# A graph layer with residual and layer norm on one core: one PSUM tile per bank, a relu on each of two engines, register loads behind long operations, 101 copied groups

## The chip, the core and the metric

The kernel runs on one core of a Trainium2 chip. The metric is the device time of one execution in microseconds, here 1737.42 us as the median of three runs (1736.82 to 1737.85). The engines are named as in the profile: PE (matmul), PEld (its weight load), DVE (vector), ACT (scalar), POOL (GpSimd) and SP (sync, which only issues transfers).

## What is computed

The reference is one step of message passing over 12500 nodes of 64 values and 200000 edges of 32 values, then a residual and a layer norm. `col` (the destinations, `dst`) is sorted.

```python
msg_in = jnp.concatenate([nodes[row], nodes[col], edge_features], axis=-1)
messages = relu(msg_in @ mW1 + mb1) @ mW2 + mb2
aggregated = jax.ops.segment_sum(messages, col, num_segments=12500)
upd_in = jnp.concatenate([nodes, aggregated], axis=-1)
x = _layernorm(x + relu(upd_in @ uW1 + ub1) @ uW2 + ub2)
```

All of it is float32. mW1 is 160x128, mW2 128x64, uW1 128x128 and uW2 128x64.

## The kernel before

The edges are cut into 1563 tiles of 128. Six tiles make a group, here called a step: there are 261 steps (0 to 260), and two of them make a super-group g. A step's number is s, and j is 0 or 1 for the first or second step of its super-group.

**Sources.** The product of all nodes with the first 64 rows of mW1 is written to a table in DRAM early on (`tab_a`). For each tile POOL gathers the 128 rows of its sources from that table with one indirect transfer (line 209) into a ring of nine buffers `xg`. The first ten steps gather x itself and are transposed and multiplied. POOL's gathers are issued in the order of the steps, each as soon as its buffer is free.

**Copied groups.** In the steps of the list `COPIED` only four of the six tiles are gathered. The x columns of the sources of the other two tiles are copied inside SBUF, one column at a time, into a tile `xc` (64 rows for each tile), and PE multiplies them with mW1's rows (line 370). 96 steps are copied before: 16, 19, 21, 24 and so on, every 2.5 steps to 254. For each of the 128 columns a register holds the address in `xtop`, another that in `xbot`. ACT makes 64 of the 128 columns (`singly`, line 338, an add through the bias), DVE the other 64 (`joined`, line 345, a bitwise or). The addresses come from SBUF by register loads (`addresses`, line 315), at most eight columns at a time, on the same engine's queue. The work for a copied step is spread evenly over the 2.5 steps before it, and in a step DVE's part is split in two (j = 1) or three (j = 0) portions at fixed places in the order.

**Destinations and edges.** PE multiplies, for each tile, a 64-row operand `l` (32 rows of a one-hot selection of destinations, 32 of edge features) with `rhs` (32 rows of the destination table `tab_b`, 32 of mW1) into the PSUM tile `pc` (line 367). `select` makes the one-hot rows on DVE (lines 235 and 237) and a second selection `sel` (line 243) once per super-group. 

**The step.** `node_part(s)` adds the gathered rows to `pc` on DVE into `h` (line 394; line 390 in a copied step, four tiles only), and ACT applies the relu (lines 395, 391 and 392). Then `collect(s-1)` sums h by destination with PE into `sums` (line 427) and counts edges (line 424), `edge_part(s+1)` fills the next `pc`, and DVE and ACT make their portions of copies. `pc` is a tile of two PSUM banks, with two buffers.

**Updates.** 34 times in the run a period of up to 448 nodes is closed: ACT copies `sums` (lines 441, 442), SP loads the x columns of its nodes (`columns`, line 457), PE multiplies (`update`, lines 464, 465, and `residual`, lines 478, 480), ACT applies the relu (line 470), and DVE and ACT do the layer norm (lines 494 to 510). `update` and `residual` each take a buffer of `pc`. The last period begins at step 258. For it `columns` is called in step 260, at the place of the other calls, and its transfer stands behind those that SP has been given before.

The order of instructions on every engine is the order in which this code writes them; nothing is reordered.

Of the kernel before, what the change touches and what calls it, by code (L numbers as in the profile page):

```python
# [17 lines left out]
P = 128  # L18
# [6 lines left out]
SUB = 6  # L25
# [47 lines left out]
FIRST, GAPS = 16, (3, 2)  # L73
COPIED = []
while FIRST + sum(GAPS) * (len(COPIED) // len(GAPS)) + sum(GAPS[:len(COPIED) % len(GAPS)]) < NSUB - 6:
    COPIED.append(FIRST + sum(GAPS) * (len(COPIED) // len(GAPS)) + sum(GAPS[:len(COPIED) % len(GAPS)]))
RNDS = -(-len(COPIED) // len(GAPS))
LAST = 4 * (N - 1)
ACTS, CHUNK = 64, 8
# [22 lines left out]
def gnn_kernel(ctx: ExitStack, tc: tile.TileContext, x1T, x, eT, e_rows, src, src_row, dst, dst_row, wlist, wrow, wnext, whalf,  # L102
# [40 lines left out]

    cols = const.tile([RNDS * len(GAPS), 2 * P], I32, name="cols")
    col_a = const.tile([RNDS * len(GAPS), P, 2], I32, name="col_a")
# [68 lines left out]
    with tc.tile_pool(name="sup", bufs=2) as sup, tc.tile_pool(name="work", bufs=2) as work, tc.manual_schedule():  # L214
# [73 lines left out]
        def columns_list():  # L288

            for r in range(len(GAPS)):  # L290
                v = src_row[:, ((FIRST + sum(GAPS[:r])) * SUB + SUB - 2) * P:]
                nc.sync.dma_start(cols[r * RNDS:(r + 1) * RNDS],
                                  bass.AP(v.tensor, v.offset, [[sum(GAPS) * SUB * P, RNDS], [1, 2 * P]]))
            cv = cols.rearrange("k (b e) -> k b e", b=2)
            for b, base in enumerate((XBASE, YBASE)):
                nc.vector.tensor_scalar(col_a[:, :, b], cv[:, b], 4.0, float(base), op0=ALU.mult, op1=ALU.add)
# [3 lines left out]
        def portion(s, total, unit):  # L300

            rate, found = sum(GAPS) / len(GAPS), []
            begin = min(c - 2 - (j + 1) * rate for j, c in enumerate(COPIED[:len(GAPS)]))
            for j, c in enumerate(COPIED):
                lo, hi = (min(-(-int(total * (s + d - begin - j * rate) / rate * 16 + 0.5) // (16 * unit)) * unit, total) for d in (0, 1))
                lo = max(lo, 0)
                if lo < hi:
                    if c not in xc:
                        xc[c] = work.tile([P, P], F32, name="xc")
                    found.append((xc[c], j % len(GAPS) * RNDS + j // len(GAPS), lo, hi))  # L310
            return found

        def addresses(k, a, m, engine):

            _, v = nc.values_load_multi_w_load_instructions(  # L315
                col_a.rearrange("k e b -> k (e b)")[k:k + 1, 2 * a:2 * m], engines=[engine], min_val=XBASE,
                max_val=YBASE + LAST, skip_runtime_bounds_check_because="sources are node numbers")
# [15 lines left out]
        def singly(s, part, of):  # L333

            todo = [(o, k, e) for o, k, lo, hi in portion(s, ACTS, 2) for e in range(lo, hi, 2)]
# [4 lines left out]
        def joined(s, part, of):  # L340

            todo = [(o, k, ACTS + e) for o, k, lo, hi in portion(s, P - ACTS, 2) for e in range(lo, hi, 2)]
            for o, k, a, m in share(todo, part, of):
                for e, top, bot in addresses(k, a, m, ET.DVE):
                    nc.vector.tensor_tensor(o[:, e:e + 1].bitcast(I32), top.bitcast(I32), bot.bitcast(I32),  # L345
                                            op=ALU.bitwise_or)
# [9 lines left out]
        def edge_part(s):  # L356

            n = len(tiles(s))
            g, j = divmod(s, SUP // SUB)

            pc = psum.tile([P, 2, 4, DH], F32, name="pc")[:, :, :SUB // 2]
            for i in range(n):
                k, b = divmod(i, 2)
                q, m = 64 * b, j * SUB // 2 + k
                w = m if shared(g) == 1 else (j * SUB + i) // shared(g)
                copied = s in COPIED and i >= SUB - 2
                nc.tensor.matmul(pc[:, b, k, :], L[g][q:q + 64, m, :], rhs[g % 2][q:q + 64, w, :],  # L367
                                 start=s >= XG or k == 0, stop=s >= XG and not copied)
                if copied:
                    nc.tensor.matmul(pc[:, b, k, :], xc[s][q:q + 64], w1a[q:q + 64], start=False, stop=True)  # L370
            pcs[s] = pc

        def node_part(s):
# [3 lines left out]
            h = work.tile([P, 2, SUB // 2, DH], F32, name="h")  # L377
            if s < XG:
                xt = xs.pop(s)
                for i in range(n):  # L380
                    k, b = divmod(i, 2)
                    q = 64 * b
                    nc.tensor.matmul(pc[:, b, k, :], xt[q:q + 64, k, :], w1a[q:q + 64], start=False,
                                     stop=i + 2 >= n)
                nc.scalar.activation(h, pc, AF.Relu)
            else:
                a = xg.pop(s)[0].rearrange("p (b k) f -> p b k f", b=2)
                if s in COPIED:
                    m = SUB // 2 - 1
                    nc.vector.tensor_tensor(h[:, :, :m], pc[:, :, :m], a[:, :, :m], op=ALU.add)  # L390
                    nc.scalar.activation(h[:, :, :m], h[:, :, :m], AF.Relu)  # L391
                    nc.scalar.activation(h[:, :, m:], pc[:, :, m:], AF.Relu)
                for b, m in parts(n) if s not in COPIED else []:
                    nc.vector.tensor_tensor(h[:, b, :m], pc[:, b, :m], a[:, b, :m], op=ALU.add)  # L394
                    nc.scalar.activation(h[:, b, :m], h[:, b, :m], AF.Relu)  # L395
# [9 lines left out]
        def collect(s):  # L405
# [20 lines left out]
            for i in range(n):  # L426
                nc.tensor.matmul(ps[:, bass.ds(ws[i], WIN)], h[:, i % 2, i // 2, :], S[g][:, k0 + i, :],  # L427
# [46 lines left out]
        def residual(u):  # L474

            py = psum.tile([P, UB, D], F32, name="py", tag="sums" if u + 2 == K else "pc")
# [91 lines left out]
        def products(c, w):  # L568
            pb = psum.tile([P, 2, HB, DH], F32, name="pb", tag="pc")
            for i in range(HB):  # L570
                for h, m in spread(c):
                    if i < m:
                        nc.tensor.matmul(pb[:, h, i, :], (xbot if h else xtop)[64 * h:64 * h + 64, (c + HB * h + i) * P:(c + HB * h + i + 1) * P],  # L573
# [3 lines left out]
        def chunk_a(c):  # L577
            pb, tb = products(c, w1a)
            for h, m in spread(c):
                if h:  # L580
                    nc.vector.tensor_copy(tb[:, h, :m], pb[:, h, :m])  # L581
                else:
                    nc.scalar.copy(tb[:, h, :m], pb[:, h, :m])  # L583
# [3 lines left out]
        def chunk_b(c, into):  # L587
            pb, tb = products(c, w1b)
            n = min(NCH, NB - c)
            pf, tf = (t.rearrange("p h i f -> p (h i) f")[:, :n] for t in (pb, tb))  # L590
            nc.vector.tensor_tensor(tf, pf, b1.unsqueeze(1).broadcast_to([P, n, DH]), op=ALU.add)
# [107 lines left out]
        def weights():  # L699

            pw = psum.tile([D, DH], F32, name="pw", tag="pc")
# [3 lines left out]
            pw2 = psum.tile([DH, DH], F32, name="pw2", tag="pc")  # L705
            nc.tensor.matmul(pw2, w2T, u1a, start=True, stop=True)
            nc.vector.tensor_copy(w2u, pw2)
            pw3 = psum.tile([1, DH], F32, name="pw3", tag="pc")
# [3 lines left out]
        def checks():  # L712
# [15 lines left out]
            pf = psum.tile([1, 1], F32, name="pf", tag="pc")  # L728
# [27 lines left out]
        for s in range(last + 2):  # L756
# [13 lines left out]
            if s < NSUB:  # L770
                node_part(s)
                joined(s, 0, 3 if j == 0 and g + 1 < NSUP else 2)
# [54 lines left out]
    with tc.If(flag > 0), tc.tile_pool(name="gen", bufs=1) as up:  # L827
# [28 lines left out]
        with tc.For_i(0, NT, 1) as t:  # L856
# [26 lines left out]
            pc = psum.tile([P, DH], F32, name="pcg", tag="pc")  # L883
# [34 lines left out]
        with tc.For_i(0, NB, 1) as c:  # L918
# [7 lines left out]
            ph = psum.tile([DH, P], F32, name="phu", tag="pc")  # L926
# [66 lines left out]
```

## Time and profile before

| | before |
|---|---|
| time, median of three runs | 1737.42 us |
| time of the profiled execution | 1741.59 us |
| its span, first to last instruction | 1739.8 us |
| granted TensorE clock, mean | 0.581 |
| PE busy | 1448.5 us, 83% |
| PEld busy | 1247.5 us, 72% |
| DVE busy | 1056.2 us, 61% |
| ACT busy | 1468.6 us, 84% |
| POOL busy | 1301.0 us, 75% |
| gathers on POOL (line 209) | 1371 |
| copies on ACT (line 338) and DVE (line 345) | 6144 each |
| register loads on DVE and ACT (line 315) | 1055 and 912 |

The span is counted from the first to the last instruction; 1.8 us of the profiled execution lie around it. The profiled execution took 4.2 us more than the median of the runs. Busy time leaves out register loads, waits on semaphores and the issue of transfers, which an engine's sequencer does. In the tables of groups the numbers behind the bar are the busy time of the group, the mean of one instruction in ns, and the idle time of the engine just before, with what ended it. "issue" stands for idle time that ended without any wait in the profile.

### The profile page before, as it was taken

How to read it: one execution, taken by the hardware profiler on the slowest of the kernel's cores; microseconds unless marked ns; L12 is line 12 of the kernel's file. 1: busy time of each engine (PE TensorE's matmuls, PEld its weight loads, DVE VectorE, ACT ScalarE, POOL GpSimd, SP SyncE). 2: the span in 40 equal slices, each digit the busy share in tenths (PEclk: the TensorE clock that was granted, in tenths of full speed). 3: DMA queues.
4: the chain of work that ended last, by engine and by line, in shares of the span. 5: the costliest groups of instructions: out<-in, count | busy, mean ns of one | idle time of the engine just before them, and what ended most of it. 6: DMA issues, size and time to landing. Idle time of an engine off the chain costs nothing.

```text
span 1739.8 us, 46406 instructions
## 1 busy us (share of the span) xinstructions
PE 1448.5 (83%) x9620; PEld 1247.5 (72%) x9620; DVE 1056.2 (61%) x7329; ACT 1468.6 (84%) x6712; POOL 1301.0 (75%) x1380
## 2 busy tenths in 40 slices
PE   3697888888988888887987898888899878899997
PEld 3586777877777767666776776677777767677776
DVE  1526666666665656666665666666667666666643
ACT  0277989999998898998898999998999999899942
POOL 7777777777777777777777777777777777777774
PEclk8585555555555555656555555655556566666656
DMA  8783444433333333333343433443344444443442
GB/s 213 204 175 99 127 112 115 115 97 100 98 101 92 96 97 93 98 102 94 98 107 102 105 108 103 105 107 103 106 106 110 107 109 106 108 112 104 113 112 66
DMA packets 207588, 192.45 MB, mean 111 GB/s; under 512 B 57511, under 2 KB 173409, under 8 KB 207313
## 3 DMA queue, kind: packets, MB, share of 16 engines
q0 software_dynamic: 43872, 87.97, 20.6%
q1 hardware_dynamic: 148896, 92.56, 19.6%
q10 hardware_dynamic: 14546, 8.93, 1.8%
q8 instruction: 91, 1.49, 0.4%
q14 instruction: 183, 1.50, 0.3%
HBM read 171.54 MB, written 17.76 MB: 109 GB/s over the span
## 4 chain that ended last, share of the span: by engine, by line
POOL 41%; issue 24%; DMA 14%; DVE 10%; PE 5%; ACT 2%; DVEq 2%; SPq 1%; ACTq 0%; POOLq 0%
POOL xg L209 41%; DMA xg<-tab_a,src_s 10%; DVE xc L345 3%; DVE h L394 2%; ACT xc L338 2%; PE sums L427 2%; DVEq L315 2%; PE pc L367 1%; DVE l L237 1%; DMA tab_a<-tb 1%; DMA l<-in_dst_row 1%; DMA w1b<-in_mW 1%; DVE h L390 0%; DMA l<-in_eT 0%; DMA xtop<-in_x1T 0%
## 5 line engine op out<-in xcount | busy, mean ns | idle before, releaser
L209 POOL DMA_INDIRECT xg<-tab_a,src_s x1311 | 1242.0, 947 | 399.8 <-issue 372.0
L338 ACT ACTIVATE xc<-xtop,xbot 128x1 f32 x6144 | 1166.2, 280 | 42.2 <-issue 31.7
L345 DVE TENSOR_TENSOR xc<-xtop,xbot 128x1 int32 x6144 | 536.6, 154 | 417.9 <-issue 402.4
L427 PE MATMUL sums<-sel,h 128*128 128x32 f32 x3126 | 638.9, 371 | 20.4 <-ACT h L395 13.9
L427 PEld LDWEIGHTS sums<-sel,h 128*128 128x128 f32 x3126 | 605.3, 294 | 39.1 <-ACT h L395 15.4
L367 PE MATMUL pc<-rhs,l 64*128 64x128 f32 x3126 | 420.0, 415 | 188.7 <-DVE h L394 134.7
L367 PEld LDWEIGHTS pc<-rhs,l 64*128 64x128 f32 x3126 | 349.6, 295 | 253.0 <-DVE h L394 152.3
L395 ACT ACTIVATE h<-h 128x768 f32<-128x768 f32 x156 | 129.6, 831 | 111.6 <-DVE h L394 110.8
L394 DVE TENSOR_TENSOR h<-pc,xg 128x768 f32<-128x768 f32 x156 | 148.0, 949 | 121.8 <-DMA xg<-tab_a,src_s 67.6
L237 DVE TENSOR_TENSOR l<-l,cps 128x768 f32<-128x768 int32 (+1 forms) x134 | 127.8, 953 | 23.4 <-DMA l<-in_dst_row 18.8
L424 PEld LDWEIGHTS <-one 128*1 128x1 bf16 x1563 | 55.9, 83 | 58.7 <-issue 50.7
L424 PE MATMUL cnt<-sel,one 128*1 128x32 bf16 x1563 | 89.2, 187 | 0.4 <-issue 0.3
L390 DVE TENSOR_TENSOR h<-pc,xg 128x512 f32<-128x512 f32 x96 | 66.1, 688 | 25.8 <-DMA xg<-tab_a,src_s 11.5
L243 DVE TENSOR_TENSOR sel<-cps,drc 128x384 f32<-128x384 f32 x131 | 71.6, 547 | 14.9 <-PE sums L427 14.7
L464 PE MATMUL pu<-xw,uz 128*128 128x448 f32 (+1 forms) x68 | 61.8, 1012 | 17.3 <-DVE h L394 13.6
L370 PE MATMUL pc<-w1a,xc 64*128 64x128 f32 x384 | 75.0, 398 | 0.0
L209 POOL DMA_INDIRECT xg<-in_x,src_s x60 | 58.0, 967 | 19.1 <-issue 17.7
L391 ACT ACTIVATE h<-h 128x512 f32<-128x512 f32 x96 | 59.2, 617 | 10.4 <-DVE h L390 9.5
L370 PEld LDWEIGHTS pc<-w1a,xc 64*128 64x128 f32 x384 | 66.7, 311 | 0.0
L583 ACT COPY tb<-pb 128x512 f32<-128x512 f32 (+1 forms) x13 | 7.4, 570 | 58.5 <-DMA tab_a<-tb 26.1
L465 PE MATMUL pu<-sums_s,w2u 128*128 128x448 f32 (+1 forms) x68 | 55.2, 914 | 0.0
L573 PE MATMUL pb<-w1a,xtop 64*128 64x128 f32 x100 | 24.0, 425 | 29.9 <-DVE tb L581 17.9
(104 smaller groups left out, 803.3 us busy)
## 6 DMA issues: line engine op xcount, KB each, us to landing
l<-in_dst_row SPq DMA_DIRECT2D x262, 96.0 KB
l<-in_eT SPq DMA_DIRECT2D x262, 96.0 KB
xg<-tab_a,src_s POOLq DMA_INDIRECT x1311
rhs<-tab_b SPq DMA_DIRECT2D x361, 32.0 KB
tab_b<-tb SPq DMA_DIRECT2D x13, 512.0 KB
rhs<-tab_b SPq DMA_DIRECT2D x387, 16.0 KB
tab_a<-tb ACTq DMA_DIRECT2D x12, 512.0 KB
out<-y SPq DMA_DIRECT2D x33, 128.0 KB
```

What stands on the lines that cost most here:

```text
L209: nc.gpsimd.indirect_dma_start(out=a[:, i, :] if s < XG else a[:, i // 2, i % 2, :], out_offset=None, in_=A[:, :] if s >= XG else x[:, :], ...
L237: nc.vector.tensor_tensor(l[r], l[r].bitcast(I32), node[r].unsqueeze(2).broadcast_to([r.stop - r.start, SUP // 2, P]), op=ALU.is_equal)
L243: nc.vector.tensor_tensor(s[:, :nt], slot.unsqueeze(1).broadcast_to([P, nt, WIN]), drc[:, g * SUP:g * SUP + nt].unsqueeze(2).broadcast_to( ...
L338: nc.scalar.activation(o[:, e:e + 1], top.bitcast(F32), AF.Identity, bias=bot.bitcast(F32))
L345: nc.vector.tensor_tensor(o[:, e:e + 1].bitcast(I32), top.bitcast(I32), bot.bitcast(I32), op=ALU.bitwise_or)
L367: nc.tensor.matmul(pc[:, b, k, :], L[g][q:q + 64, m, :], rhs[g % 2][q:q + 64, w, :], start=s >= XG or k == 0, stop=s >= XG and not copied)
L370: nc.tensor.matmul(pc[:, b, k, :], xc[s][q:q + 64], w1a[q:q + 64], start=False, stop=True)
L390: nc.vector.tensor_tensor(h[:, :, :m], pc[:, :, :m], a[:, :, :m], op=ALU.add)
L394: nc.vector.tensor_tensor(h[:, b, :m], pc[:, b, :m], a[:, b, :m], op=ALU.add)
L395: nc.scalar.activation(h[:, b, :m], h[:, b, :m], AF.Relu)
L424: nc.tensor.matmul(pn[:, bass.ds(ws[i], WIN)], one, SB[g][:, k0 + i, :, 1], start=False, stop=ends and i == n - 1)
L427: nc.tensor.matmul(ps[:, bass.ds(ws[i], WIN)], h[:, i % 2, i // 2, :], S[g][:, k0 + i, :], start=False, stop=ends and i == n - 1)
```

## The change

- The list of copied groups follows a curve, `progress`, rather than fixed gaps: 0.43 groups a step at first and 0.41 at the end. It gives 101 steps (16, 18, 20, 23 to 254). The work for them runs from step 11 to step 251.
- ACT makes 66 of the 128 columns, DVE 62. There are three buffers of `xc`. The addresses of all steps are prepared, where before only those of copied steps were.
- `pc` becomes two tiles of one bank, `pc0` and `pc1`, and `h` two tiles of half the size. DVE adds each half by itself. ACT applies the relu to the first half, DVE (a `tensor_scalar` with max) to the second. In the second half, and in copied steps in the first, the sum stays in PSUM and the relu writes h.
- DVE's register loads are taken apart from its copies (`fetch` and `join`): four columns are loaded right behind each add (two behind the second one in a copied step) and behind the relu, eight behind line 237, four behind the second selection; what is left of a step's columns follows at the step's end, eight at a time.
- The update takes `pc0`, the residual `pc1`; the products for the tables take one of each. The addition of the bias to the second table is split by bank.
- `columns` of the last period is called at the end of step 258, no longer in step 260.

```diff
-FIRST, GAPS = 16, (3, 2)
+BEGIN, FINAL = 11, 255
+RATES = 0.43, 0.41
+SWING = 0.0
+def progress(s, early=0.0):
+    s = max(s + 1 - BEGIN, 0)
+    return s * (RATES[0] + (RATES[1] - RATES[0]) * s / (2 * NSUB)) + (early if s else 0.0)
...
+for s in range(NSUB):
+    while min(progress(s), progress(s, -SWING if s % 2 else SWING)) >= len(COPIED) + 1 and s + 3 < FINAL:
+        COPIED.append(s + 3)
...
-ACTS, CHUNK = 64, 8
+ACTS, CHUNK = 66, 8
...
             if at is not None:
-                joined(at, 1, 3)
+                join(fetch(quota(at), 8))
             s = sup.tile([P, SUP, WIN], F32, name="sel")
...
+            if at is not None:
+                join(fetch(quota(at), 4))
...
+        def fetch(todo, n):
+            ready = []
+            while todo and n:
+                o, k, a = todo[0]
+                m = min(len([t for t in todo if t[1] == k]), n // 2)
+                del todo[:m]
+                n -= 2 * m
+                ready += [(o, *x) for x in addresses(k, a, a + 2 * m, ET.DVE)]
+            return ready
...
-            pc = psum.tile([P, 2, 4, DH], F32, name="pc")[:, :, :SUB // 2]
+            pc = [psum.tile([P, 4, DH], F32, name=f"pc{b}")[:, :SUB // 2] for b in range(2)]
...
-                if s in COPIED:
-                    m = SUB // 2 - 1
-                    nc.vector.tensor_tensor(h[:, :, :m], pc[:, :, :m], a[:, :, :m], op=ALU.add)
-                    nc.scalar.activation(h[:, :, :m], h[:, :, :m], AF.Relu)
-                    nc.scalar.activation(h[:, :, m:], pc[:, :, m:], AF.Relu)
-                for b, m in parts(n) if s not in COPIED else []:
-                    nc.vector.tensor_tensor(h[:, b, :m], pc[:, b, :m], a[:, b, :m], op=ALU.add)
-                    nc.scalar.activation(h[:, b, :m], h[:, b, :m], AF.Relu)
+                m = SUB // 2 - (s in COPIED)
+                todo = quota(s)
+                if n == SUB:
+                    o = pc[0] if s in COPIED else h[0]
+                    nc.vector.tensor_tensor(o[:, :m], pc[0][:, :m], a[:, 0, :m], op=ALU.add)
+                    nc.scalar.activation(h[0], o, AF.Relu)
+                    ready = fetch(todo, 4)
+                    nc.vector.tensor_tensor(pc[1][:, :m], pc[1][:, :m], a[:, 1, :m], op=ALU.add)
+                    ready += fetch(todo, 2 if s in COPIED else 4)
+                    nc.vector.tensor_scalar(h[1], pc[1], 0.0, None, op0=ALU.max)
+                    join(ready + fetch(todo, 4))
...
-            pu = psum.tile([DH, UN], F32, name="pu", tag="pc")[:, :n]
+            pu = psum.tile([DH, UN], F32, name="pu", tag="pc0")[:, :n]
...
-            if s + 2 in due:
+            if s + 2 in due and due[s + 2] + 1 < K:
                 columns(due[s + 2])
+            if s == UPD[K - 1]:
+                columns(K - 1)
             rest(s)
-            joined(s, 2 if j == 0 and g + 1 < NSUP else 1, 3 if j == 0 and g + 1 < NSUP else 2)
+            while s < NSUB and quota(s):
+                join(fetch(quota(s), CHUNK))
             singly(s, 0, 1)
```

More of the change, by code (lines that the diff above doesn't have):

```diff
@@ L142, in gnn_kernel @@
     past = const.tile([1, 1], F32, name="past")
-    cols = const.tile([RNDS * len(GAPS), 2 * P], I32, name="cols")
-    col_a = const.tile([RNDS * len(GAPS), P, 2], I32, name="col_a")
+    col_a = const.tile([P, 2, P, 2], I32, name="col_a")
     w1b = const.tile([P, DH], F32, name="w1b")
@@ L288, in columns_list, with portion @@
         def columns_list():
[L290 to L296, printed above, removed]
+            cols = work.tile([P, 2, 2, P], I32, name="cols", tag="tb")
+            for r in range(2):
+                n = min(P, NSUB - 1 - r * P)
+                v = src_row[:, (r * P * SUB + SUB - 2) * P:]
+                nc.sync.dma_start(cols[:n, r].rearrange("k b e -> k (b e)"),
+                                  bass.AP(v.tensor, v.offset, [[SUB * P, n], [1, 2 * P]]))
+                for b, base in enumerate((XBASE, YBASE)):
+                    nc.vector.tensor_scalar(col_a[:n, r, :, b], cols[:n, r, b], 4.0, float(base), op0=ALU.mult, op1=ALU.add)
         x8, y8 = xtop.bitcast(U8), xbot.bitcast(U8)
-        def portion(s, total, unit):
-            rate, found = sum(GAPS) / len(GAPS), []
-            begin = min(c - 2 - (j + 1) * rate for j, c in enumerate(COPIED[:len(GAPS)]))
+        def portion(s, total, early=(0.0, 0.0)):
+            found = []
             for j, c in enumerate(COPIED):
-                lo, hi = (min(-(-int(total * (s + d - begin - j * rate) / rate * 16 + 0.5) // (16 * unit)) * unit, total) for d in (0, 1))
-                lo = max(lo, 0)
+                lo, hi = (min(max(int((progress(s + d, early[d + 1]) - j) * total / 2 + 1e-6) * 2, 0), total) for d in (-1, 0))
                 if lo < hi:
                     if c not in xc:
-                        xc[c] = work.tile([P, P], F32, name="xc")
-                    found.append((xc[c], j % len(GAPS) * RNDS + j // len(GAPS), lo, hi))
+                        xc[c] = work.tile([P, P], F32, name="xc", bufs=3)
+                    found.append((xc[c], c, lo, hi))
             return found
@@ L315, in addresses @@
             _, v = nc.values_load_multi_w_load_instructions(
-                col_a.rearrange("k e b -> k (e b)")[k:k + 1, 2 * a:2 * m], engines=[engine], min_val=XBASE,
+                col_a[k % P:k % P + 1, k // P].rearrange("k e b -> k (e b)")[:, 2 * a:2 * m], engines=[engine], min_val=XBASE,
                 max_val=YBASE + LAST, skip_runtime_bounds_check_because="sources are node numbers")
@@ L333, in singly @@
         def singly(s, part, of):
-            todo = [(o, k, e) for o, k, lo, hi in portion(s, ACTS, 2) for e in range(lo, hi, 2)]
+            todo = [(o, k, e) for o, k, lo, hi in portion(s, ACTS) for e in range(lo, hi, 2)]
             for o, k, a, m in share(todo, part, of):
@@ L338, in singly, with quota, join @@
                     nc.scalar.activation(o[:, e:e + 1], top.bitcast(F32), AF.Identity, bias=bot.bitcast(F32))
[L340 to L346, printed above, removed]
+        def quota(s):
+            if s not in quotas:
+                quotas[s] = [(o, k, ACTS + e) for o, k, lo, hi in portion(s, P - ACTS) for e in range(lo, hi, 2)]
+            return quotas[s]
+        def fetch(todo, n):
[7 more added lines that the diff above has]
+            return ready
+        def join(ready):
+            for o, e, top, bot in ready:
+                nc.vector.tensor_tensor(o[:, e:e + 1].bitcast(I32), top.bitcast(I32), bot.bitcast(I32),
+                                        op=ALU.bitwise_or)
+        quotas = {}
         xc = {}
@@ L366, in edge_part @@
                 copied = s in COPIED and i >= SUB - 2
[L367 removed]
+                nc.tensor.matmul(pc[b][:, k, :], L[g][q:q + 64, m, :], rhs[g % 2][q:q + 64, w, :],
                                  start=s >= XG or k == 0, stop=s >= XG and not copied)
                 if copied:
[L370 removed]
+                    nc.tensor.matmul(pc[b][:, k, :], xc[s][q:q + 64], w1a[q:q + 64], start=False, stop=True)
             pcs[s] = pc
@@ L376, in node_part @@
             pc = pcs.pop(s)
-            h = work.tile([P, 2, SUB // 2, DH], F32, name="h")
+            h = [work.tile([P, SUB // 2, DH], F32, name=f"h{b}") for b in range(2)]
             if s < XG:
@@ L474, in residual @@
         def residual(u):
-            py = psum.tile([P, UB, D], F32, name="py", tag="sums" if u + 2 == K else "pc")
+            py = psum.tile([P, UB, D], F32, name="py", tag="sums" if u + 2 == K else "pc1")
             for i in range(blocks(u)):
@@ L568, in products @@
         def products(c, w):
-            pb = psum.tile([P, 2, HB, DH], F32, name="pb", tag="pc")
+            pb = [psum.tile([P, HB, DH], F32, name=f"pb{h}", tag=f"pc{h}") for h in range(2)]
             for i in range(HB):
@@ L572, in products @@
                     if i < m:
-                        nc.tensor.matmul(pb[:, h, i, :], (xbot if h else xtop)[64 * h:64 * h + 64, (c + HB * h + i) * P:(c + HB * h + i + 1) * P],
+                        nc.tensor.matmul(pb[h][:, i, :], (xbot if h else xtop)[64 * h:64 * h + 64, (c + HB * h + i) * P:(c + HB * h + i + 1) * P],
                                          w[64 * h:64 * h + 64], start=True, stop=True)
@@ L580, in chunk_a @@
                 if h:
-                    nc.vector.tensor_copy(tb[:, h, :m], pb[:, h, :m])
+                    nc.vector.tensor_copy(tb[:, h, :m], pb[h][:, :m])
                 else:
-                    nc.scalar.copy(tb[:, h, :m], pb[:, h, :m])
+                    nc.scalar.copy(tb[:, h, :m], pb[h][:, :m])
             n = min(NCH, NB - c)
@@ L589, in chunk_b @@
             n = min(NCH, NB - c)
-            pf, tf = (t.rearrange("p h i f -> p (h i) f")[:, :n] for t in (pb, tb))
-            nc.vector.tensor_tensor(tf, pf, b1.unsqueeze(1).broadcast_to([P, n, DH]), op=ALU.add)
+            for h, m in spread(c):
+                nc.vector.tensor_tensor(tb[:, h, :m], pb[h][:, :m], b1.unsqueeze(1).broadcast_to([P, m, DH]), op=ALU.add)
+            tf = tb.rearrange("p h i f -> p (h i) f")[:, :n]
             for v in into:
@@ L771, in gnn_kernel @@
                 node_part(s)
-                joined(s, 0, 3 if j == 0 and g + 1 < NSUP else 2)
             if s in at_end:
```

26 lines of the change are left out of this document (14 added, 12 removed).

## The prediction

> **What bounds the kernel now.** I read the page's chain and its groups first, then POOL's rows, then the waits of each engine by stage, and last the sequencer rows of DVE and the timeline of the end.
>
> ```profile
> POOL 41%; issue 24%; DMA 14%; DVE 10%; PE 5%; ACT 2%; DVEq 2%; SPq 1%; ACTq 0%; POOLq 0%
> ...
> L209 POOL DMA_INDIRECT xg<-tab_a,src_s x1311 | 1242.0, 947 | 399.8 <-issue 372.0
> ...
> L209 POOL DMA_INDIRECT xg<-in_x,src_s x60 | 58.0, 967 | 19.1 <-issue 17.7
> ```
>
> The chain lies on POOL and on the "issue" gaps between its gathers. One gather is 947 ns and the gap before the next 0.3 us. In the timeline the 1371 gathers start at 2.85 and end at 1720.6: one each 1.2531 us, with no start-to-start interval over 1.33 us behind the first hundred. POOL never waits, so POOL's count of gathers sets the end, as long as the consumers of a group (a "step" of six tiles) keep up. Do they? From the same timeline, DVE's add of step 10 starts 33 us behind POOL's last gather of that step, and the distance shrinks to 28 us at step 25, 20 at step 50 and 3.7 at step 70, and stays at 2 to 4 us from there. So until about 480 us the consumers run at their own pace: 6.11 us a step (step 15 at 157.3, step 55 at 401.7), then 5.63 (step 70 at 486.2). POOL's pace is 5.2 gathers x 1.2531 = 6.52.
>
> What sets the consumers' own pace is read where nothing else holds them, from 390 to 480 us (first the busy time of PE, PEld, DVE, ACT and POOL with counts, then DVE's waits there, then its register loads over the whole run):
>
> ```profile
> 390.00:480.00 90.00, 80.49 (x517) 71.41 (x516) 62.24 (x450) 89.41 (x434) 68.13 (x72) 0.53 0.37 98
> ```
>
> ```profile
> DVE xc L345 <- issue: 24.8, 55, 1.0
> DVE h L394 <- PE pc L367: 0.5, 1, 0.5
> ```
>
> ```profile
> L315 DVEq TENSOR_LOAD <-col_a x1055: 341/883/2359, 122.2 to 1667.0; - x176
> ```
>
> ACT is full there (89.41 of 90), and so is DVE: 62.2 busy, and nearly all of the rest is "issue", the time in which DVE's sequencer reads column addresses into registers (L315) ahead of the L345 copies. The change puts more on exactly this queue, so DVE's sequencer is the second thing to cost. Taken in order, the 1055 loads are the fetches that the loops write, and their medians by size are 0.351, 0.608, 0.867 and 1.125 us for 2, 4, 6 and 8 columns. From a load's end to the next load it is 0.157, 0.222, 0.292 and 0.364 us with so many copies between: 0.087 and 0.035 a copy. DVE itself needs 0.072 a copy, so it lags and catches up under the next load. A load behind an add runs beside it:
>
> ```profile
> 908.35 0.96 DVE L394 TENSOR_TENSOR h<-pc,xg 128x768 f32<-128x768 f32 x1
> ...
> 909.57 0.69 DVE L345 TENSOR_TENSOR xc<-xtop,xbot 128x1 int32 x8 [0.26 <-issue]
> ```
>
> **POOL: fewer gathers.** The new list has 101 copied groups for 96; each spares two gathers. 1361 x 1.2531 against 1371: -12.5 us, on the path.
>
> **The end.** The chain's last stretch waits for x's columns:
>
> ```profile
> 1725.95 0.56 ACT L442 COPY sums_s<-sums 128x480 f32<-128x480 f32 x1 [0.23 <-PE sums L427]
> 1727.57 0.40 SPq L457 DMA_DIRECT2D xw<-in_x1T  x1
> ...
> 1729.58 1.19 PE L464 MATMUL pu<-xw,uz 128*128 128x256 f32 x2 [3.66 <-DMA xw<-in_x1T]
> ```
>
> SP issues that load behind the store of the update before. Issued from step 258, some ten us sooner, it has landed; next late is ACT's L442, which ends at 1726.5. L465, which reads it, starts at 1730.6 now and could at about 1727.3: -3.2 us (-1.9, the load's own flight, to -3.7, the whole wait). SP carries the load ahead of that store; the store of an earlier update costs the end nothing.
>
> **ACT.** Copies: 6666 x 0.190 (1166.2 / 6144) against 6144: +99 us. Relus: now 128.9 + 59.2 + 34.8 = 223; then 250 of 128x384 at about 0.48 (0.471 for the 128x384 copy L285; 0.362 and 0.617 for 256 and 512): 120. Net -4. At the early rate of 0.43 groups a step, 28.4 copies x 0.19 + 0.48 and up to 0.4 of updates make 5.9 to 6.3 a step. POOL then needs 5.14 x 1.2531 = 6.44. ACT keeps up, with little left.
>
> **DVE's engine.** Two adds of 128x384 at 0.554 (between 0.424 for 256 and 0.957 for 768) for one of 0.957; a relu from PSUM at about 0.55 (0.689 for the 512 copy L581); 118 more copies. That is near 185 us more busy time, 1056 to 1240 of 1720. Each add and the relu has a load of four columns right behind it, 0.608, which is longer than the operation: so they cost the queue nothing. Without that cover they would cost 250 x 1.66 = 415 us against the 1.24 per step that add and load take now.
>
> **DVE's sequencer, the cost that decides.** Over steps 11 to 251:
> - Loads: 215, 166, 171 and 503 of 2, 4, 6 and 8 columns now, 230, 795, 81 and 267 then (1373). By the medians 891 and 935 us: +0.18 a step.
> - Copies between loads: three loads of a step now share one row of copies: 883 rows for 1055, -11 us, -0.05 a step.
> - Waits: four semaphore instructions, 0.095 apart, precede an add now, 0.33 a step net. Two adds and a relu need some five, and a turn-round behind each load: I take 0.61, +0.28 a step. Bounds: -0.1, if the sequencer passes the next operation on while a load runs, to +0.6, if each operation waits for all that the one add waits for. In between, because the two adds share the gathers' semaphores.
> - L237 waits for the copies ahead of it to drain: 0.35 behind 2 copies, 0.56 behind 8, so 0.70 behind 12: +0.31 every other step, +0.16.
>
> Sum +0.57 a step. Queued behind these waits on DVE are the copies, the selections and the statistics; who waits is PE (the second half of h, the next group's l) and ACT's first relu, which now comes after half an add, sooner than before.
>
> So DVE's pace becomes 6.11 + 0.57 = 6.68 up to step 55 (122 + 44 x 6.68 = 416 us), then 5.63 + 0.57 with 0.07 for denser updates (95 x 6.27, 1012 us at step 150), then 6.40 (updates, about 1.5 us of DVE each, come every 5 steps rather than every 17), 101 steps: 1658 us at step 251. POOL ends step 251's gathers at 2.85 + 1312 x 1.2531 = 1647. DVE is 11 us late there; the last nine steps have no copies, POOL needs 49 x 1.25 = 61 us for them and DVE under 45. Up to 16 us are made good, so POOL still sets the end. The margin is small: 0.03 us a step. The ring of nine row buffers holds: the consumers may be about 51 us behind (32 behind with 19 to spare at step 17) and reach 35 to 40.
>
> **PE.** 20 more matmuls, about 4 us, off the path. Its waits for banks (L367 behind L394, 134.7 us) shrink as an update takes one bank and no longer two; nothing on the path is gained.
>
> **The sum.** The profiled execution: span 1739.8, time 1741.59, 4.2 above the median of 1737.42. Span 1739.8 - 12.5 - 3.2 = 1724.1; on the median's scale 1737.4 - 15.7 = 1721.7, say 1722.
>
> **Rules that bear on it.** The gathers of the trace take 947 ns whatever DVE does, also beside the 132 SBUF-to-SBUF scalings of L510 (0.33 us each). [...] No run here shows a relu on DVE.
>
> **Rivals.**
> 1. DVE's sequencer becomes the bound, and the kernel slower. The place is the stretch from the first add to the end of the relu; the price is 0.1 to 0.25 us a step over my sum (semaphores on each of three operations, instruction stalls like the 2022 ns load at 174.7). From 0.03 a step on, DVE sets the end, and each 0.1 is 24 us: 0.1 gives 1722 + 24 - 7 = 1739, 0.15 gives 1751, 0.2 gives 1763. For it: DVE is full already from 180 to 480 us. Against: DVE's adds now wait 79 us for gathers (67.6 and 11.5 in the waits), nearly all behind 470 us, and twelve columns a step are loaded under operations.
> 2. DVE late by a little only, 0.03 to 0.07 a step: 1724 to 1734.
> 3. POOL held up by the relus: 250 x 0.55 = 137 us, 1859. The steady gathers speak against it.
> 4. The queue reads on during a load, so the waits cost nothing. DVE then has 0.3 a step to spare, and the time is again 1722: it does not lower POOL's floor.
> 5. The columns come no sooner, because SP is held up: 1725.
>
> **How the numbers follow.** POOL bound, 1719 to 1725 (cases 4 and 5 in it): 0.50. Rival 2: 0.15. Rival 1: 0.32, of which 0.06 lands within 0.2% and 0.26 above. Rival 3: 0.02; 0.01 is left for the unforeseen on the fast side. A measurement of this kernel can tell about 0.2%, 3.5 us, from no change. Faster 0.66, same 0.06, slower 0.28. The range goes from 1717 (the whole wait at the end, and a little) to 1761, near rival 1 at 0.2 a step; the likeliest case alone is 1717 to 1727.
>
> **What would show it.** Right: 1361 gathers at 1.25 us with no waits; the add of step 260 some 2 us behind the last gather; DVE 10 to 45 us behind POOL from step 50 to 251; L464 at the end released by ACT; L315 near 1373 loads of 0.6 median; the idle "issue" of L345 below 402 us. Wrong: POOL's groups with waits for DVE (the ring full), DVE's add over 50 us behind POOL, or gathers longer than 947 ns.

## The result, and the profile after

The changed kernel takes 1746.97 us (median of four runs, 1743.85 to 1748.42) for 1737.63 before: a ratio of 1.005, 95% interval 1.0038 to 1.0062. It is slower by half a per cent. The forecast was 1722; the time lies in the range (1717 to 1761) but on the side to which I had given 0.28: I had forecast a gain of 15.7 us, and the kernel lost 9. The outcome is that of the first rival. The profiled execution took 1746.58 us and its span is 1744.8. In seven of the runs of the study the kernel before itself took 2503 to 2539 us; they tell nothing of the change, and stand at the end of the experiments.

POOL did what was forecast. These are its two groups on the page after, in the same columns as before:

```profile
L218 POOL DMA_INDIRECT xg<-tab_a,src_s x1301 | 1228.7, 944 | 396.5 <-issue 357.2
...
L218 POOL DMA_INDIRECT xg<-in_x,src_s x60 | 58.9, 981 | 19.1 <-issue 17.7
```

There are 1361 gathers, one each 1.2508 us, with the same small gaps. In the timeline the last one ends at 1704.9, 15.7 us sooner than before. But the span ends 39.9 us after it, where before it was 19.2. What was behind POOL? The distance from POOL's last gather of a step to DVE's first add of that step, read from the timelines, in us:

| step | 15 | 30 | 55 | 100 | 150 | 200 | 251 | 259 |
|---|---|---|---|---|---|---|---|---|
| before | 32.7 | 25.7 | 16.8 | 2.2 | 2.8 | 2.4 | 5.2 | 1.8 |
| after | 35.9 | 40.2 | 43.7 | 39.2 | 35.4 | 33.2 | 34.1 | 21.9 |

Before, DVE catches up with POOL by step 75. After, it falls back until step 55 and never catches up: POOL runs ahead within its nine buffers and waits for nobody (no wait over 0.3 us), and DVE sets the end. From 390 to 480 us, the stretch that was shown of before, the busy times and DVE's waits are these:

```profile
390.00:480.00 90.00, 74.79 (x468) 68.10 (x468) 64.73 (x452) 85.06 (x429) 68.05 (x73) 0.50 0.35 92
```

```profile
DVE xc L370 <- issue: 17.5, 39, 1.1
DVE pc L423 <- issue: 3.7, 11, 0.6
DVE h L425 <- DVE pc L423: 1.0, 6, 0.2
DVE pc L423 <- PE pc L394: 0.7, 1, 0.7
DVE pc L423 <- DMA xg<-tab_a,src_s: 0.3, 1, 0.3
```

ACT is no longer full (85.06 of 90, 89.41 before). DVE is busy 64.73 and idle for "issue" 21.2; it waits for other engines about a microsecond. A step takes 6.2 to 6.6 us around that stretch rather than 5.6 to 6.1. In the register loads the plan shows (the columns are minimum, median and maximum in ns, first and last start):

```profile
L325 DVEq TENSOR_LOAD <-col_a x1373: 341/609/1980, 121.4 to 1677.8; - x197
```

They are 1373, as counted, and mostly of four columns. In the timeline of DVE they stand beside the operations, as the gaps tell:

```profile
900.11 0.55 DVE L420 TENSOR_TENSOR h<-pc,xg 128x384 f32<-128x384 f32 x1
900.80 0.57 DVE L423 TENSOR_TENSOR pc<-pc,xg 128x384 f32<-128x384 f32 x1
901.52 0.56 DVE L425 TENSOR_SCALAR h<-pc 128x384 f32<-128x384 f32 x1
902.24 0.92 DVE L370 TENSOR_TENSOR xc<-xtop,xbot 128x1 int32 x12 [0.16 <-issue]
903.08 0.21 DVE L244 TENSOR_SCALAR cps<-wh,pidx 128x6 f32<-128x6 int32 x1
903.33 0.95 DVE L246 TENSOR_TENSOR l<-l,cps 128x768 f32<-128x768 int32 x1
904.55 0.65 DVE L370 TENSOR_TENSOR xc<-xtop,xbot 128x1 int32 x8 [0.26 <-issue]
```

The 0.70 us from one add to the next and the 0.72 from the second add to the relu are set by a load of four columns (0.60 each) and the time from its end to the next operation (0.26 and 0.09), not by the operations (0.55 and 0.57). Across the run the next load starts 0.281 us (median) after the first one's end where the second add stands between, and 0.116 where the relu does.

### The profile page after: what moved, and what is told of

Its sections match the earlier page's. It is cut to its first block, busy times and chain, and to the rows that moved or that the text cites. A ratio compares the mean times of both kernels' runs of the same rounds, so it can differ in the third digit from the quotient of the medians.

```text
span 1744.8 us, 48015 instructions
## 1 busy us (share of the span) xinstructions
PE 1501.0 (86%) x9640; PEld 1294.6 (74%) x9640; DVE 1214.1 (70%) x7971; ACT 1472.7 (84%) x7138; POOL 1288.6 (74%) x1370
## 4 chain that ended last, share of the span: by engine, by line
## 5 line engine op out<-in xcount | busy, mean ns | idle before, releaser
L348 ACT ACTIVATE xc<-xtop,xbot 128x1 f32 x6666 | 1264.7, 280 | 87.1 <-issue 75.0
L370 DVE TENSOR_TENSOR xc<-xtop,xbot 128x1 int32 x6262 | 525.6, 153 | 288.7 <-issue 279.7
L462 PE MATMUL sums<-sel,h 128*128 128x32 f32 x3126 | 657.1, 377 | 22.4 <-ACT h L421 19.6
L462 PEld LDWEIGHTS sums<-sel,h 128*128 128x128 f32 x3126 | 621.7, 301 | 44.1 <-ACT h L421 23.4
L394 PE MATMUL pc<-rhs,l 64*128 64x128 f32 x3126 | 443.2, 417 | 165.7 <-DMA l<-in_eT 50.3
L423 DVE TENSOR_TENSOR pc<-pc,xg 128x384 f32<-128x384 f32 (+1 forms) x250 | 128.0, 512 | 83.7 <-issue 47.9
L425 DVE TENSOR_SCALAR h<-pc 128x384 f32<-128x384 f32 x250 | 139.4, 557 | 28.2 <-DVE pc L423 17.7
L421 ACT ACTIVATE h<-h 128x384 f32<-128x384 f32 x149 | 76.6, 514 | 53.4 <-DVE h L420 51.8
L420 DVE TENSOR_TENSOR h<-pc,xg 128x384 f32<-128x384 f32 x149 | 82.4, 553 | 13.2 <-PE pc L394 10.0
L421 ACT ACTIVATE h<-pc 128x384 f32<-128x384 f32 x101 | 47.8, 474 | 14.2 <-DVE pc L420 12.8
L513 PE MATMUL py<-ux,xw 128*128 128x64 f32 x268 | 52.4, 359 | 2.3 <-DVE h L425 1.1
```

The lines of the kernel that those rows point to most:

```text
L394: nc.tensor.matmul(pc[b][:, k, :], L[g][q:q + 64, m, :], rhs[g % 2][q:q + 64, w, :], start=s >= XG or k == 0, stop=s >= XG and not copied)
L420: nc.vector.tensor_tensor(o[:, :m], pc[0][:, :m], a[:, 0, :m], op=ALU.add)
L421: nc.scalar.activation(h[0], o, AF.Relu)
L423: nc.vector.tensor_tensor(pc[1][:, :m], pc[1][:, :m], a[:, 1, :m], op=ALU.add)
L425: nc.vector.tensor_scalar(h[1], pc[1], 0.0, None, op0=ALU.max)
L462: nc.tensor.matmul(ps[:, bass.ds(ws[i], WIN)], h[i % 2][:, i // 2, :], S[g][:, k0 + i, :], start=False, stop=ends and i == n - 1)
```

## The experiments

All but the seven at the end are compared with the kernel before at 1737.6 to 1738.0 us, run beside them.

**Two columns to or from ACT.** Theory A says that DVE's sequencer sets the pace, B that PE does, C that ACT does.

```diff
-ACTS, CHUNK = 66, 8
+ACTS, CHUNK = 68, 8
```

> The changed kernel with 68 of 128 columns copied by ACT and 60 by DVE (66 and 62). Theory A (DVE's sequencer sets the consumers' pace): 0.84 columns a step fewer on DVE, 0.163 us each, is 0.14 us a step; the add of step 251 comes some 33 us sooner and POOL sets the end: 1722 to 1730 us. Theory C (ACT sets it): 0.84 columns more on ACT at 0.19 us, up to 38 us slower, 1750 to 1785. Theory B (PE sets it, waiting for the edge rows or its banks): 1747, unchanged.

Measured: 1722.24 us (1720.26 to 1724.05), ratio 0.9908 (0.9891 to 0.9924). The distance from POOL falls from 37 us at step 55 to 4.4 at step 251 and 0.7 at step 259, and DVE's adds wait for gathers again. This is the group of the first add on its page:

```profile
L420 DVE TENSOR_TENSOR h<-pc,xg 128x384 f32<-128x384 f32 x149 | 82.5, 554 | 29.6 <-DMA xg<-tab_a,src_s 15.9 <-PE pc L394 5.9 <-issue 4.0
```

The other way, `ACTS = 64`:

> The changed kernel with 64 columns on ACT and 64 on DVE. Theory A: 0.14 us a step more on DVE, 33 us over the run: 1772 to 1785. Theory C: ACT has less, 1715 to 1735. Theory B: 1747.

Measured: 1783.09 us (1782.05 to 1785.67), 1.0263 (1.0246 to 1.028). The ring of buffers is full from step 100 on (a distance of 50 us) and POOL itself waits for DVE:

```profile
POOL xg L218 <- DVE pc L423: 26.2, 31, 2.2
```

So two columns of 128 are worth 25 us in one direction and 36 in the other, with the sign that only A gives. One column a step costs DVE 0.17 to 0.23 us by the paces of steps 70 to 100 (6.21, 6.35 and 6.54 us with 60, 62 and 64 columns); I had 0.163.

**One load in place of three.**

```diff
-                    ready = fetch(todo, 4)
                     nc.vector.tensor_tensor(pc[1][:, :m], pc[1][:, :m], a[:, 1, :m], op=ALU.add)
-                    ready += fetch(todo, 2 if s in COPIED else 4)
                     nc.vector.tensor_scalar(h[1], pc[1], 0.0, None, op0=ALU.max)
-                    join(ready + fetch(todo, 4))
+                    join(fetch(todo, 8))
```

> The changed kernel with the register loads of the first half of a step in one piece: both adds, DVE's relu, then one load of eight columns and its copies. Theory A: one or two loads a step fewer and no turn-round behind a load ahead of the second add and the relu, 0.2 to 0.35 us a step less, so POOL sets the end: 1722 to 1730. The idea of the change (loads beside long operations are free): the load lies beside the relu only, 0.5 us a step more, 1800 to 1860. Theories B and C: 1747.

Measured: 1846.88 us (1846.27 to 1849.4), 1.0624 (1.0607 to 1.0642). My theory of fewer loads fell: there are 1028 of them rather than 1373, and the kernel is 100 us slower. The other expectation, 1800 to 1860 us with the load beside the relu only, held. The timeline shows why:

```profile
901.47 0.55 DVE L420 TENSOR_TENSOR h<-pc,xg 128x384 f32<-128x384 f32 x1
901.93 0.56 DVE L422 TENSOR_TENSOR pc<-pc,xg 128x384 f32<-128x384 f32 x1
902.52 0.56 DVE L423 TENSOR_SCALAR h<-pc 128x384 f32<-128x384 f32 x1
903.78 0.69 DVE L370 TENSOR_TENSOR xc<-xtop,xbot 128x1 int32 x8 [0.70 <-issue]
```

The load of eight begins only when the relu does, at 902.54, and the relu waits for the second add (901.93 to 902.49). The first two operations, 1.06 us, then cover no load. Loads beside operations are what makes the split bearable.

**The list alone**, in the kernel before: `COPIED`, `progress`, the columns' portions and three buffers of `xc` from the change; relus, banks and the three-part `joined` as before, 64 columns on each engine.

> The kernel before with only the new list of 101 copied groups (64 columns each on ACT and DVE, the relus all on ACT, its own portions of copies, three buffers of xc). Theory A: DVE needs some 0.2 us a step more than before, 5.85 to 6.1, less than POOL's 6.45: the ten gathers are saved, 1724 to 1730 us. Theory C (ACT must be relieved of half the relus first): ACT needs 5.1 for copies, 0.89 for relus and 0.15 to 0.45 for updates, 6.1 to 6.45, with its waits for the adds 6.5 or more: 1737 to 1760.

Measured: 1724.93 us (1724.61 to 1725.08), 0.9923 (0.9907 to 0.994). The list needs nothing of the rest. DVE and ACT run at 6.1 us a step from step 70 to 150, the upper end of what I expected from DVE (5.85 to 6.1). ACT is 98% busy there and DVE waits for almost nothing but its register loads (from 300 to 900 us 176.3 us of idle "issue" ahead of its copies, and some 9 us for anything else), so both are near their limits; they reach POOL at step 175.

**The columns alone**, in the kernel before:

```diff
-            if s + 2 in due:
+            if s + 2 in due and due[s + 2] + 1 < K:
                 columns(due[s + 2])
+            if s == UPD[K - 1]:
+                columns(K - 1)
```

> The kernel before with only the last period's x columns loaded at step 258. My sum: 3.2 us less (1.9 to 3.7), 1734 to 1736 us. From the end of the run with 68 columns on ACT, where the first matmul of the last update is no longer released by that load: 15.8 us from the last gather to the end for 19.2 before, so 3.4. Rival (the load only changes places with another wait, ACT's copy of sums): under 1 us, 1737 to 1738.

Measured: 1734.01 us (1732.07 to 1736.05), 0.9978 (0.9969 to 0.9987): 3.7 us gained, the upper bound of my term. In the changed kernel too the first matmul of the last update no longer waits for the load, and ACT's copy of sums is next late:

```profile
1724.25 0.36 SPq L492 DMA_DIRECT2D xw<-in_x1T  x1
...
1735.29 1.20 PE L499 MATMUL pu<-xw,uz 128*128 128x256 f32 x2
1735.52 0.56 ACT L477 COPY sums_s<-sums 128x480 f32<-128x480 f32 x1 [0.87 <-PE sums L462]
1736.13 0.50 PEld L500 LDWEIGHTS pu<-sums_s,w2u 128*128 128x128 f32 x2 [0.36 <-ACT sums_s L477]
```

**List and columns**, without the split of banks and relus, the moved loads and the 66 columns:

> The kernel before with the list of 101 and the sooner columns: all of the change but the split of banks and relus, the moved loads and the 66 columns. If the two gains add up: 1724.9 - 2.5 to 3.4, 1721 to 1723 us, what I forecast for the whole change. If the split were needed for part of it: 1724 to 1728.

Measured: 1723.32 us (1721.82 to 1723.82), 0.9916 (0.9902 to 0.9929). The two gains nearly add up. What is left out costs the changed kernel 23.7 us (1746.97 - 1723.32). With 64 columns on each engine in both kernels, the split of banks and relus with its moved loads costs more than twice that: 59.8 us (1783.09 - 1723.32). The two columns that went to ACT made good 36 of it.

**The split with the old number of groups**: the changed kernel with `RATES = 0.4, 0.4` and `ACTS = 64`.

> The changed kernel with the rate of 0.40 throughout (96 groups) and 64 columns on each engine as before: the banks, the relus, the loads and the sooner columns without the longer list. Theory A (DVE's sequencer): 25.6 columns a step on DVE for 26.0, pace 6.3 to 6.45 from step 55 on, POOL's 6.50; the distance shrinks slowly from 40 us and is nearly gone at the end: 1734 to 1742 us, DVE's add of step 251 at most 15 us behind POOL's gathers. Theory D (the split of banks and relus by itself costs nothing and only the ten groups overload DVE): DVE reaches POOL by step 100, 1734 to 1736.

Measured: 1733.29 us (1732.63 to 1735.21), 0.9974 (0.9964 to 0.9985), no other than the columns alone. DVE's distance from POOL is 30 us at step 55, 15 at step 100 and 3 at step 175: later than before (step 75), as A expects, but in time. The split costs DVE pace, and that costs time only when POOL is quicker.

**More groups**: list and columns with `RATES = 0.43, 0.44`, 104 groups.

> The same with rates of 0.43 to 0.44, 104 copied groups, 1355 gathers. POOL's floor is three groups lower, 6 x 1.2508 = 7.5 us: 1714 to 1716 if DVE and ACT, both full at 6.1 us a step up to step 150 in the kernel with the list alone, still catch up with POOL (6.37 to 6.43). If not, they set the end: 1718 to 1730.

Measured: 1724.1 us (1722.71 to 1725.75), 0.9924 (0.991 to 0.9937). POOL ends at 1696.6, 8.5 us sooner than with 101 groups, but the distance stays near 20 us from step 150 to 251: DVE and ACT set the end (from 1000 to 1600 us ACT is busy 592.7 of 600, and DVE's idle time is nearly all "issue"). 104 groups bring no more than 101.

**The second relu back on ACT**, in the changed kernel:

```diff
-                    nc.vector.tensor_scalar(h[1], pc[1], 0.0, None, op0=ALU.max)
+                    nc.scalar.activation(h[1], pc[1], AF.Relu)
```

> The changed kernel with the relu of the second half on ACT too (both relus there), the rest unchanged: two banks, two adds with loads behind them, 66 columns on ACT. Theory E (the relu on DVE lies under a load and costs DVE little; it is there to relieve ACT): ACT needs 0.47 us a step more, 6.2 + 0.47 = 6.65, and becomes the bound: 1790 to 1820 us, ACT's idle time near nothing. Theory F (the relu on DVE is what makes DVE late, 0.56 us a step): DVE falls under POOL's pace and the time goes to 1722 to 1730.

Measured: 1763.09 us (1759.52 to 1768.38), 1.014 (1.0123 to 1.0157). From 600 to 1600 us the busy times of PE, PEld, DVE, ACT and POOL are, in the changed kernel and in this one:

```profile
600.00:1600.00 1000.00, 898.18 (x5598) 765.19 (x5598) 737.99 (x5069) 926.63 (x4596) 756.17 (x801) 0.57 0.40 105
```

```profile
600.00:1600.00 1000.00, 909.92 (x5528) 778.45 (x5529) 645.05 (x4869) 968.93 (x4712) 755.94 (x801) 0.55 0.40 104
```

DVE loses 93 us of work there and is no quicker. Its idle time for register loads grows by as much ("issue" ahead of the copies from 180.2 to 282.0 us), since the load that lay beside the relu is now bare. These are the groups of the copies over the whole run, the changed kernel's and this one's:

```profile
L370 DVE TENSOR_TENSOR xc<-xtop,xbot 128x1 int32 x6262 | 525.6, 153 | 288.7 <-issue 279.7
```

```profile
L370 DVE TENSOR_TENSOR xc<-xtop,xbot 128x1 int32 x6262 | 525.9, 153 | 439.7 <-issue 434.7
```

Theory F falls. E holds in its sign and its mechanism (ACT is 96.9% busy); its size was 16 us and not 43 or more. ACT had 73 us idle in these 1000 us of the changed kernel and has 31 here, so its idle time took up much of the second relu.

**The seven other runs.** They are of five of the kernels above, with the same expectations. All lie within 0.4% of the kernel before (here 2503 to 2539 us), whatever was changed, and in the first of them POOL waits 672 us for DVE's adds (471.3 and 200.9), where in the kernel before it waits for none of them longer than 0.3 us; what sets the time there was not followed up. These runs decide between no theories. The columns alone, 2528.64 us against 2521.51 (1.0027, 0.9999 to 1.0056):

> The kernel before with only the last period's x columns loaded at step 258. My sum: 3.2 us less (1.9 to 3.7), 1734 to 1736 us. From the end of the run with 68 columns on ACT, where the first matmul of the last update is no longer released by that load: 15.8 us from the last gather to the end for 19.2 before, so 3.4. Rival (the load only changes places with another wait, ACT's copy of sums): under 1 us, 1737 to 1738.

The split with the old number of groups, 2532.15 us (1.0033, 0.9994 to 1.0073):

> The changed kernel with the rate of 0.40 throughout (96 groups) and 64 columns on each engine as before: the banks, the relus, the loads and the sooner columns without the longer list. Theory A (DVE's sequencer): 25.6 columns a step on DVE for 26.0, pace 6.3 to 6.45 from step 55 on, POOL's 6.50; the distance shrinks slowly from 40 us and is nearly gone at the end: 1734 to 1742 us, DVE's add of step 251 at most 15 us behind POOL's gathers. Theory D (the split of banks and relus by itself costs nothing and only the ten groups overload DVE): DVE reaches POOL by step 100, 1734 to 1736.

List and columns, 2528.25 us (1.0019, 0.9988 to 1.005):

> The kernel before with the list of 101 and the sooner columns: all of the change but the split of banks and relus, the moved loads and the 66 columns. If the two gains add up: 1724.9 - 2.5 to 3.4, 1721 to 1723 us, what I forecast for the whole change. If the split were needed for part of it: 1724 to 1728.

More groups, 2524.46 us (1.0008, 0.9983 to 1.0032):

> The same with rates of 0.43 to 0.44, 104 copied groups, 1355 gathers. POOL's floor is three groups lower, 6 x 1.2508 = 7.5 us: 1714 to 1716 if DVE and ACT, both full at 6.1 us a step up to step 150 in the kernel with the list alone, still catch up with POOL (6.37 to 6.43). If not, they set the end: 1718 to 1730.

The second relu on ACT, three times: 2534.63 us against 2538.93 (0.999), 2502.87 against 2502.69 (1.0011) and 2526.47 against 2524.43 (1.0012):

> The changed kernel with the relu of the second half on ACT too (both relus there), the rest unchanged: two banks, two adds with loads behind them, 66 columns on ACT. Theory E (the relu on DVE lies under a load and costs DVE little; it is there to relieve ACT): ACT needs 0.47 us a step more, 6.2 + 0.47 = 6.65, and becomes the bound: 1790 to 1820 us, ACT's idle time near nothing. Theory F (the relu on DVE is what makes DVE late, 0.56 us a step): DVE falls under POOL's pace and the time goes to 1722 to 1730.

> The changed kernel with the relu of the second half on ACT too (both relus there), the rest unchanged: two banks, two adds with loads behind them, 66 columns on ACT. Theory E (the relu on DVE lies under a load and costs DVE little; it is there to relieve ACT): ACT needs 0.47 us a step more, 6.2 + 0.47 = 6.65, and becomes the bound: 1790 to 1820 us, ACT's idle time near nothing. Theory F (the relu on DVE is what makes DVE late, 0.56 us a step): DVE falls under POOL's pace and the time goes to 1722 to 1730.

> The changed kernel with the relu of the second half on ACT too (both relus there), the rest unchanged: two banks, two adds with loads behind them, 66 columns on ACT. Theory E (the relu on DVE lies under a load and costs DVE little; it is there to relieve ACT): ACT needs 0.47 us a step more, 6.2 + 0.47 = 6.65, and becomes the bound: 1790 to 1820 us, ACT's idle time near nothing. Theory F (the relu on DVE is what makes DVE late, 0.56 us a step): DVE falls under POOL's pace and the time goes to 1722 to 1730.

## Why the prediction was wrong

**Right.** POOL's 10 gathers fewer: 1361 at an even pace, its end 15.7 us sooner. I had 12.5, and the ten gathers are worth that much: the other 3 us belong to the profiled execution of before, which took 4.2 us more than its median, at 1.2531 us a gather. In the run with the columns alone the same 1371 gathers come at 1.2509 and end at 1717.6, 12.7 us behind the changed kernel's. The columns at the end: 3.7 against 3.2. The relu on DVE lies under its load (0.557 us under 0.608; without it, in the last experiment, DVE's idle time grew by what its work lost). No relu held POOL up: the gathers did not lengthen (944 ns for 947), and the 299 that ran beside a relu on DVE took 944 ns in the median and 957 at most. The number of loads and their lengths: their sum is 947 us and was 914 before; I had 935 and 891. The floor itself: the runs with 68 columns (1722.2) and with list and columns (1723.3) stand where I put the change, 1722.

**Wrong: the sum over DVE's steps, which was to be 11 us behind POOL at step 251, with 16 to make good.** The +0.57 us a step held as a sum (of its terms only the loads were measured by themselves): DVE runs at 6.63 us from step 15 to 55 (I had 6.68) and at 6.17 from 55 to 70 (5.63 + 0.57 is 6.20). What failed is the pace of before that it was added to, most of all in the first four steps.

| stretch | forecast us | measured us |
|---|---|---|
| steps 11 to 15 | 26.7 | 39.2 |
| steps 15 to 55 | 267 | 265 |
| steps 55 to 150 | 596 | 601 |
| steps 150 to 251 | 646 | 651 |
| steps 251 to 259 | under 40 | 45 |

The first row is the term that failed: 12.5 us. I multiplied the pace of steps 15 to 55 from step 11 on. But steps 11 to 15 hold work that is done once, the products of the weights and the checks on DVE. They take 8.8 us each before as well (35.1 us), which the two times in my own text, 122 at step 11 and 157.3 at step 15, would have told. In DVE's timeline the work lies between two portions of copies, in the kernel before and in the changed one:

```profile
138.08 0.37 DVE L345 TENSOR_TENSOR xc<-xtop,xbot 128x1 int32 x4 [0.29 <-issue]
140.43 0.28 DVE L704 COPY w2T<-pw 64x128 f32<-64x128 f32 x1 [1.98 <-PE pw L702]
...
142.77 1.76 DVE L717 TENSOR_REDUCE mm<-drc 128x1 f32<-128x1563 f32 x1
144.46 1.76 DVE L718 TENSOR_REDUCE mm<-drc 128x1 f32<-128x1562 f32 x1
...
149.40 0.65 DVE L345 TENSOR_TENSOR xc<-xtop,xbot 128x1 int32 x8 [1.07 <-issue]
```

```profile
139.58 0.97 DVE L370 TENSOR_TENSOR xc<-xtop,xbot 128x1 int32 x12 [0.33 <-issue]
142.46 0.28 DVE L740 COPY w2T<-pw 64x128 f32<-64x128 f32 x1 [1.91 <-PE pw L738]
...
151.13 0.65 DVE L370 TENSOR_TENSOR xc<-xtop,xbot 128x1 int32 x8 [1.10 <-issue]
```

That is some 10 us in each (138.45 to 148.33 and 140.55 to 150.03, without the load ahead of the last copies) in which DVE works on no step. In the changed kernel the step that holds it takes 15.7 us from first add to first add (137.08 to 152.81), 9 more than my 6.68.

The second term is the pace behind step 70, where before DVE waited for POOL and did not show its own. It is 6.36 us from step 70 to 150 and 6.44 from 150 to 251, for 6.27 and 6.40: 10 us over in the two rows, 0.05 us a step. I had added 0.07 for denser updates from step 55 on, and the pace rises by 0.19 (6.36 for 6.17); that the updates alone make this is not shown. The last steps run at 5.65 us and not at 5. With POOL 3 us quicker than forecast, DVE is 34 us behind at step 251, for 11, and makes good 12 by step 259.

**What I should have said.** With the 12.5 us in it, the same sum has DVE some 23 us late with 16 to make good, and the time about 7 us over the floor, near 1729 (an estimate from the numbers above). And with a margin of 0.03 us a step and a pace good to 0.05, 0.50 for POOL as the bound was too much. The first rival had the bound and the sign, and its 1739 (0.1 a step) and 1751 (0.15) stand around the measured 1747. But half of the lateness came from the once-only work, which it did not name; the steps behind step 55 cost 0.05 us over my sum, less than its 0.1 to 0.25, and no run shows that this is paid between the first add and the relu, nor what made the 2.022 us load that it named long. That its time came out near is in part luck.

**Rival 4**, that the queue reads on while a load runs, is not what the traces show: the second add begins a median of 0.26 us after the end of the load ahead of it and never before that end, and none of the 407 semaphore instructions that stand ahead of the second adds starts inside a load.

## What to carry to other kernels

When one engine's pace is the bound and the others follow close behind, cost what the change adds to each follower, its sequencer included, over every stretch of the run, the once-only work at the start among them; the slack a stage shows in its waits is what may be spent. Where an engine copies through addresses in registers, count its register loads (here 947 us on DVE, for 526 us of copies), and put a load behind each operation of its length: the relu of 0.557 us was free here with a load of 0.608 behind it, while one load behind two adds and the relu lay beside the relu alone, and the kernel was 100 us slower. Before a whole package is kept or dropped, run its parts alone: here the list and the sooner columns give 0.8%, and the rest loses it.

## What the runs showed of the hardware that I had not expected

- A register load on DVE took 0.351 us for four registers, 0.608 for eight, 0.867 for twelve and 1.125 for sixteen (medians before), about 0.064 us for each register and 0.09 besides. In the changed kernel it ran beside the operation ahead of it (900.83 to 901.43, the second add 900.80 to 901.37), and what stood behind it was held back: none of DVE's 1091 semaphore instructions starts inside a load, and no second add and no relu before the end of the load ahead of it. The relu started a median of 0.09 us after that end, the second add, which has semaphore instructions ahead of it, 0.26.
- The load behind the relu, which waits for the second add on its own engine, started 0.013 to 0.024 us after the relu in the changed kernel (238 loads) and 0.015 us after it in the step shown of the run with one load (902.54). Of 241 loads behind the first add 108 started before the add did, by up to 0.81 us.
- Moving 0.56 us of work a step off DVE gained DVE nothing (idle "issue" 279.7 to 434.7 us), and moving 0.84 columns a step, 0.07 us of its busy time, gained 0.14 us (6.21 for 6.35 from step 70 to 100).
